# Layer 0 of a four-layer graph network: a hand-written order, one load per row tile, and the neighbour lists of two row tiles built later

## The chip, the cores and the metric

The kernel runs on one core of one Trainium2 chip. The number is device microseconds of one execution. The core has a matrix engine (TensorE, PE in the profile, its weight loads PEld), a vector engine (VectorE, DVE), an activation engine (ScalarE, ACT), a general engine (GpSimd, POOL), and a queue engine (SyncE, SP) that starts most transfers. Each works through its own instructions in order and waits on the others by semaphores.

## The reference, cut to what matters

`x` is 2708 x 128 and `adj` is 2708 x 2708, both float32. About 16 entries in a row of `adj` are not zero. Four layers follow each other, each of the form "normalise, ReLU, graph layer, add":

```python
# layer 0: aggregation over columns
h = relu(layernorm(x));  x = x + (adj.T @ h) / adj.sum(axis=0)[:, None]
# layer 1: one message for every pair (i, j), weighted with adj
h = relu(layernorm(x))
messages = gelu(s[:, None, :] + d[None, :, :] + msg_b)     # s, d: two linear maps of h
aggregated = einsum('ijd,ij->id', messages, adj)
x = x + layernorm(gelu(linear(h, aggregated)) + h)
# layer 2: adj @ h into a GRU cell;   layer 3: two heads of masked attention over adj
```

In layer 1 only the pairs with a non-zero entry count, so the kernel makes lists of these entries instead of computing 2708 x 2708 messages.

## The kernel before, in words

The rows of `adj` are cut into 22 row tiles of 128 (the last has 20), and the row tiles into six groups of four (`GROUPS`; the last group has tiles 20 and 21). The columns are cut into 22 blocks of `JB` = 124.

**Layer 0 (lines 227 to 290)** passes once over `adj` and does four things with each row tile:

- It adds to `adj.T @ h` on TensorE: six matmuls per tile into six PSUM banks (line 250).
- It lists the tile on VectorE: for each of the 22 blocks, line 269 (`nc.vector.max`) takes the eight largest values of each row and line 270 (`nc.vector.max_index`) their positions. The results are `val` and `col`. The two or three blocks around the diagonal come from a copy, `near`, in which GpSimd has put zeros on the diagonal (lines 259 and 262). GpSimd also makes `dg`, the diagonal alone (line 261). `near` and `dg` have two buffers each.
- ScalarE counts the entries of each row (line 274, `sign`) and takes the diagonal out of `dg` (line 275).
- When a group is complete, its four tiles are transposed block by block on TensorE into one of two PSUM banks (line 281), ScalarE copies the bank to `aT` with column sums (line 285), and SyncE stores it to `adjT` in device memory (line 288). `aT` has eight buffers. The sums of all 132 copies give the degrees.

Two groups of `adj` are held at a time (pool `l0`, `bufs=2`). The first and the last group are loaded tile by tile (line 244), the four in between with one transfer of 5.4 MB each (line 246). `moments_apart` computes the normalisation of the rows of tiles 4 to 21 on ScalarE and GpSimd. In this layer the order on each engine is found by a scheduler from priorities.

**The start of layer 1 (lines 738 to 751)** is a written order: `spread_sums` (line 676) transposes the sums, `enter` (line 685) divides them by the degrees and adds them to `x`, `count_rows` (line 362), `rank` (lines 377 to 379), `select_rows` (line 368), and so on until the loop can start.

**Layer 1's loop** is `period(t)`, 22 periods with one row tile each and six steps `k`. It is a pipeline: period `t` computes messages of tile `t` (`combine`, lines 528 and 532, and `gather`, line 553), and prepares tiles `t + 1` to `t + 4`. On VectorE a period has, in this order: `rank(t+3)` (lines 378, 379, from a PSUM bank that several small products share), `describe(t+3)` (line 354), `sources` in even periods (line 503), `select_rows(t+3)` (line 368), `count_rows(t+4)` (line 362, reads `val`), pieces of `update`, `columns(t+1)` (line 482), `place(t+2)` (lines 420 to 443) and `finish_rows(t+3)` (line 399). The order is written out, since the whole part stands under `tc.manual_schedule()`.

Layers 2 and 3 read `adjT` again and are not touched.

Of the kernel before, what the change touches and what calls it, by code (L numbers as in the profile page):

```python
# [20 lines left out]
F32 = mybir.dt.float32  # L21
BF16 = mybir.dt.bfloat16
AF = mybir.ActivationFunctionType
ALU = mybir.AluOpType
# [6 lines left out]
P = 128  # L31
N = 2708
D = 128
NT = (N + P - 1) // P
FULL = N // P
TAIL = N - FULL * P
CH = 512
CHUNKS = [(c, min(CH, N - c)) for c in range(0, N, CH)]
# [5 lines left out]
JB = 124  # L44
NB = (N + JB - 1) // JB
S = 8
E = P
GROUPS = [(t, min(4, NT - t)) for t in range(0, NT, 4)]
# [3 lines left out]
def size(t):  # L52
    return min(P, N - t * P)


def width(b):
    return min(JB, N - b * JB)
# [3 lines left out]
def listed_layers(ctx: ExitStack, tc: tile.TileContext, x, adj, w, out, flag):  # L61
    nc = tc.nc
# [7 lines left out]
    def bank(name):  # L70
        return ps.tile([P, CH], F32, tag="ps", name=name)

    xs = const.tile([P, NT, D], F32, name="xs")
    h = const.tile([P, NT, D], F32, name="hs")
    adjT = dram.tile([P, NT, N], F32, name="adjT")
# [10 lines left out]
    ident = const.tile([P, P], F32, name="ident")  # L86
# [47 lines left out]
    def scale_rows(dst, src, rstd, shift, func):  # L134

        for q in range(len(src)):
            nc.scalar.activation(dst[q], src[q], func, bias=shift[:, q : q + 1], scale=rstd[:, q : q + 1])

    def tiles_of(v, t, k):
        return [v[:, t + q, :] for q in range(k)]  # L140
# [50 lines left out]
    for q in range(2):  # L191
        nc.gpsimd.tensor_copy(xb[q][:, :, 4 * S : 4 * S + R], part.unsqueeze(1).to_broadcast([P, NB, R]))

    sumT = keep.tile([D, N], F32, name="hT1")
    hT = sumT
    with tc.tile_pool(name="l0c", bufs=1) as fix:
        offdiag = fix.tile([P, P], F32, name="offdiag")
        nc.vector.tensor_scalar(offdiag, ident, -1.0, 1.0, ALU.mult, ALU.add)  # L200
        sums = fix.tile([P, NT, len(GROUPS)], F32, name="sums")
        nc.gpsimd.memset(sums, 1.0)

        RT = NT - 4
        flat = fix.tile([P, 4, RT], F32, name="flat")
        shifts, ve, rstd, tmp = (flat[:, q, :] for q in range(4))

        def moments_apart(pool):
            for t in range(4, NT):
                junk = pool.tile([P, D], F32, name="junk")  # L210
                nc.scalar.activation(junk, xs[:, t, :], AF.Copy, accum_out=shifts[:, t - 4 : t - 3])
            nc.gpsimd.tensor_scalar(shifts, shifts, -1.0 / D, None, ALU.mult)
            for t in range(4, NT):
                junk = pool.tile([P, D], F32, name="junk")
                nc.scalar.activation(
                    junk, xs[:, t, :], AF.Square, bias=shifts[:, t - 4 : t - 3], accum_out=ve[:, t - 4 : t - 3]
                )
            nc.gpsimd.tensor_scalar(ve, ve, 1.0 / D, EPS, ALU.mult, ALU.add)
            nc.gpsimd.tensor_tensor(rstd, ve, minus_half[:, 0:RT], ALU.pow)
            nc.gpsimd.tensor_tensor(tmp, rstd, rstd, ALU.mult)  # L220
            nc.gpsimd.tensor_tensor(tmp, tmp, ve, ALU.mult)
            nc.gpsimd.tensor_scalar(tmp, tmp, -0.5, 1.5, ALU.mult, ALU.add)
            nc.gpsimd.tensor_tensor(rstd, rstd, tmp, ALU.mult)
            nc.gpsimd.tensor_tensor(shifts, shifts, rstd, ALU.mult)
            scale_rows(tiles_of(h, 4, RT), tiles_of(xs, 4, RT), rstd, shifts, AF.Relu)

        with (
            tc.tile_pool(name="l0", bufs=2) as rows,
            tc.tile_pool(name="l0k", bufs=2) as pool,
            tc.tile_pool(name="l0t", bufs=8) as turned,  # L230
            tc.tile_pool(name="l0p", bufs=1, space=PSUM) as acc,
        ):
            accs = [acc.tile([P, CH], F32, name=f"acc{c}") for c in range(len(CHUNKS))]
            for gi, (g0, gk) in enumerate(GROUPS):
                i0, iw = span(g0, gk)
                a4 = rows.tile([P, 4, N], F32, name="a")
                if gk < 4:
                    nc.gpsimd.memset(a4[:, gk - 1, :], 0.0)
                for q in range(gk):
                    n = g0 + q  # L240
                    m = size(n)
                    a = a4[:, q, :]
                    if not 0 < gi < len(GROUPS) - 1:
                        nc.sync.dma_start(a[0:m, :], adj[n * P : n * P + m, :])
                    elif q == 0:
                        nc.sync.dma_start(a4, adj[i0 : i0 + iw, :].rearrange("(t p) n -> p t n", p=P))
                    if n == 1:
                        load_rest()
                    for ci, (c, cw) in enumerate(CHUNKS):
                        nc.tensor.matmul(  # L250
                            accs[ci][:, 0:cw], h[0:m, n, :], a[0:m, c : c + cw], start=(n == 0), stop=(n == NT - 1)
                        )

                    d0 = n * P
                    b0 = d0 // JB
                    b1 = (d0 + m - 1) // JB
                    c0, c1 = b0 * JB, min((b1 + 1) * JB, N)
                    near = pool.tile([P, 3 * JB], F32, name="near")
                    nc.gpsimd.tensor_copy(near[:, 0 : c1 - c0], a[:, c0:c1])
                    dg = pool.tile([P, P], F32, name="dg")  # L260
                    nc.gpsimd.tensor_tensor(dg[:, 0:m], a[:, d0 : d0 + m], ident[:, 0:m], ALU.mult)
                    nc.gpsimd.tensor_tensor(
                        near[:, d0 - c0 : d0 - c0 + m], a[:, d0 : d0 + m], offdiag[:, 0:m], ALU.mult
                    )
                    for b in range(NB):
                        ab = a[:, b * JB : b * JB + width(b)]
                        if b0 <= b <= b1:
                            ab = near[:, b * JB - c0 : b * JB - c0 + width(b)]
                        nc.vector.max(val[:, n, b, :], ab)  # L269
                        nc.vector.max_index(col[:, n, b, :], val[:, n, b, :], ab)  # L270
                    if n == 2:
                        moments_apart(pool)
                    sign = pool.tile([P, N], BF16, name="sign")
                    nc.scalar.activation(sign, a, AF.Sign, accum_out=total[:, n : n + 1])
                    nc.scalar.activation(dg[:, 0:m], dg[:, 0:m], AF.Copy, accum_out=own[:, n : n + 1])
                for j in range(NT):
                    k = size(j)
                    p = bank("p_T")
                    for q in range(gk):
                        m = size(g0 + q)  # L280
                        nc.tensor.transpose(  # L281
                            p[0:k, q * P : q * P + m], a4[0:m, q, j * P : j * P + k], ident[0:m, 0:m]
                        )
                    aT = turned.tile([P, CH], F32, name="aT")
                    nc.scalar.activation(  # L285
                        aT[0:k, 0:iw], p[0:k, 0:iw], AF.Copy, accum_out=sums[0:k, j, gi : gi + 1]
                    )
                    nc.sync.dma_start(adjT[0:k, j, i0 : i0 + iw], aT[0:k, 0:iw])
            for ci, (c, cw) in enumerate(CHUNKS):
                nc.scalar.copy(sumT[:, c : c + cw], accs[ci][:, 0:cw])  # L290


        deg = fix.tile([P, 3, NT], F32, name="deg")
        dsum, lim, fin = (deg[:, q, :] for q in range(3))
        nc.vector.reduce_sum(dsum, sums, AX.X)
        nc.vector.reciprocal(inv, dsum)
        nc.vector.tensor_scalar(lim, inv, FMAX, -FMAX, ALU.min, ALU.max)
        nc.vector.tensor_tensor(fin, lim, inv, ALU.is_equal)
        nc.vector.tensor_tensor(inv, lim, fin, ALU.mult)
# [30 lines left out]
    with (  # L330
# [35 lines left out]
        def compare(dst, numbers, op):  # L366

            nc.vector.tensor_tensor(  # L368
                dst.rearrange("p b (x r) -> p b x r", r=R),
                count_h.rearrange("p (x r) -> p x r", r=R).unsqueeze(1).to_broadcast([P, NB, P // R, R]),  # L370
                numbers.unsqueeze(2).to_broadcast([P, NB, P // R, R]),
                op,
            )

        def rank(t):
            p = rpool.tile([P, CH], F32, tag="r", name="p_r")
# [20 lines left out]
        def finish_rows(t):  # L397
            sel = state[t]["sel"]
            nc.vector.tensor_tensor(sel, sel, later, ALU.subtract)
# [225 lines left out]
        def period(t, between=()):  # L625
# [5 lines left out]
            for k in range(GB):  # L631
# [33 lines left out]
                    place(t + 2)  # L665
                if k == 4 and a:
                    finish_rows(t + 3)


        def spread_sums(g):  # L670
# [946 lines left out]
```

## Time and profile before

| what | us |
|---|---|
| runs, median (lowest, highest) of 3 | 1091.82 (1085.76, 1094.81) |
| the profiled execution, and its span | 1090.83, 1089.0 |
| layer 0 up to the last list on VectorE | 0 to 223.4 |
| the last transposes and copies of layer 0 | 223.4 to 234.7 |
| start of layer 1 up to the first message products | 234.7 to 294 |
| layer 1's loop and its last updates | 294 to about 640 |
| layers 2 and 3 | about 640 to 1089 |

The table is cut by hand from the timelines. In the profile a group of instructions is one line: source line, engine, operation, output and input, shapes, count; then the busy time and the mean duration in ns; then the idle time of the engine just before these instructions and who ended it. The durations of neighbouring VectorE instructions overlap by a few tens of ns, so the pace of a sequence is read from start times.

### The profile page before, as it was taken

Reading aid. Unit: us, or ns where it says so; the run is one execution under the profiler, and the core shown is the slowest. Engines: PE = TensorE matmul, PEld = TensorE weight load, DVE = VectorE, ACT = ScalarE, POOL = GpSimd, SP = SyncE. Lnnn points to the kernel's source line nnn. Section 1 sums busy time; section 2 is a strip of 40 time slices with the busy share of each in tenths; the row PEclk is TensorE's granted clock in tenths of the full one; section 3 lists DMA queues with packets and bytes.
Section 4 is the critical chain, followed back from the end, with each engine's and each line's share of the span. In section 5 each row is a group of like instructions: output and inputs, shape, how many; then the busy total and the mean of one; then the engine's idle time right before and its main releaser. Section 6 shows DMA issues by size and latency. Waiting matters only on the chain. (4 is left out here: it accounts for less than half of the span.)

```text
span 1089.0 us, 21908 instructions
## 1 busy us (share of the span) xinstructions
PE 959.5 (88%) x7950; PEld 762.3 (70%) x7950; DVE 825.6 (76%) x2856; ACT 516.0 (47%) x1431; POOL 395.7 (36%) x474
## 2 busy tenths in 40 slices
PE   6688779964599999999999979999978999999993
PEld 3355445633499999989898944444578999999762
DVE  7999999957777667776887265666578977997673
ACT  7957547745566666666675522433322200230142
POOL 4301102012486655676666253444310300340132
PEclk9798899766599999999999989999989999899996
DMA  9586786441033322222222046556400000000000
GB/s 367 182 316 239 305 320 228 181 155 54 27 108 108 108 88 102 81 102 88 96 93 82 29 174 224 188 193 223 131 27 21 11 4 1 1 20 1 1 16 14
DMA packets 56922, 128.18 MB, mean 118 GB/s; under 512 B 7458, under 2 KB 20126, under 8 KB 54096
## 3 DMA queue, kind: packets, MB, share of 16 engines
q1 hardware_dynamic: 54988, 123.89, 32.2%
q10 hardware_dynamic: 1816, 2.80, 0.9%
q8 instruction: 64, 1.05, 0.4%
q14 instruction: 54, 0.44, 0.1%
HBM read 80.07 MB, written 30.87 MB: 102 GB/s over the span
## 5 line engine op out<-in xcount | busy, mean ns | idle before, releaser
L867 PE MATMUL att<-hv,wt 128*128 128x129 f32 (+2 forms) x1936 | 243.8, 283 | 8.8 <-DVE wt L835 8.8
L867 PEld LDWEIGHTS att<-hv,wt 128*128 128x128 f32 (+2 forms) x1936 | 224.7, 192 | 25.7 <-DVE wt L835 10.1
L835 DVE SCALAR_TENSOR_TENSOR wt<-row,lift,mask 128x1024 f32<-128x1024 f32 (+5 forms) x176 | 160.2, 939 | 35.0 <-PE att L867 35.0
L452 POOL TENSOR_SCALAR put<-mine,value 128x128 f32<-128x128 bf16 x176 | 148.2, 858 | 72.4 <-DVE mine L368 70.0
L528 PE MATMUL p_m<-s,sel 128*128 128x128 bf16 x1452 | 161.6, 220 | 5.5 <-ACT g L540 5.5
L532 PE MATMUL p_m<-d,cols 124*128 124x128 bf16 (+1 forms) x1452 | 161.7, 219 | 1.4 <-DVE cols L482 1.3
L121 POOL TENSOR_TENSOR n_r<-n_r,minus_half 128x4 f32<-128x4 f32 (+1 forms) x31 | 46.1, 1488 | 304.5 <-DVE n_r L120 298.9
L250 PE MATMUL acc<-a,hs 128*128 128x512 f32 (+2 forms) x264 | 119.0, 589 | 26.6 <-DMA a<-in_adj 22.7
L553 PE MATMUL agg<-put,g 128*128 128x128 f32 (+1 forms) x968 | 135.8, 281 | 0.0
L270 DVE FIND_INDEX8 col<-val,a 128x8 uint16<-128x124 f32 (+1 forms) x441 | 118.6, 281 | 0.0
L553 PEld LDWEIGHTS agg<-put,g 128*128 128x128 f32 x968 | 118.1, 192 | 0.0
L1006 PE MATMUL p_agg<-a,hs 128*128 128x512 f32 (+2 forms) x264 | 111.0, 563 | 7.8 <-DVE u L601 4.8
L528 PEld LDWEIGHTS <-sel 128*128 128x128 bf16 x1452 | 104.2, 98 | 10.9 <-issue 7.1
L269 DVE MAX8 val<-a 128x8 f32<-128x124 f32 (+1 forms) x441 | 102.6, 273 | 2.2 <-DMA a<-in_adj 2.2
L532 PEld LDWEIGHTS <-cols 124*128 124x128 bf16 (+1 forms) x1452 | 102.4, 98 | 1.9 <-DVE cols L482 1.9
L540 ACT ACTIVATE g<-p_m 128x512 f32<-128x512 f32 x132 | 73.1, 554 | 63.4 <-PE p_m L532 63.4
L281 PEld LDWEIGHTS p_T<-ident,a 128*128 128x128 f32 x484 | 61.8, 152 | 57.7 <-ACT aT L285 34.0
L460 ACT ACTIVATE put<-mine,value 128x128 f32<-128x128 bf16 x308 | 100.4, 390 | 0.0
L281 PE MATMUL p_T<-ident,a 128*128 128x128 f32 x484 | 80.7, 302 | 19.5 <-DMA a<-in_adj 10.1
L250 PEld LDWEIGHTS acc<-a,hs 128*128 128x128 f32 (+1 forms) x264 | 48.0, 204 | 66.4 <-issue 38.6
L1006 PEld LDWEIGHTS p_agg<-a,hs 128*128 128x128 f32 (+1 forms) x264 | 48.2, 196 | 57.0 <-issue 56.0
L285 ACT ACTIVATE aT<-p_T 128x512 f32<-128x512 f32 (+2 forms) x132 | 71.0, 544 | 32.5 <-issue 13.9
(244 smaller groups left out, 1401.8 us busy)
## 6 DMA issues: line engine op xcount, KB each, us to landing
adjT<-aT SPq DMA_DIRECT2D x105, 256.0 KB
a<-adjT SPq DMA_DIRECT2D x20, 1280.0 KB
a<-in_adj SPq DMA_DIRECT2D x4, 5416.0 KB
spread<-passed SPq DMA_DIRECT2D x22, 704.0 KB
later<-sel SPq DMA_DIRECT2D x22, 616.0 KB
a<-in_adj SPq DMA_DIRECT2D x5, 1354.0 KB
row<-own_d ACTq DMA_DIRECT2D x10, 256.0 KB
later<-sel SPq DMA_DIRECT2D x22, 82.5 KB
```

The lines of the kernel that those rows point to most:

```text
L250: nc.tensor.matmul(accs[ci][:, 0:cw], h[0:m, n, :], a[0:m, c : c + cw], start=(n == 0), stop=(n == NT - 1))
L269: nc.vector.max(val[:, n, b, :], ab)
L270: nc.vector.max_index(col[:, n, b, :], val[:, n, b, :], ab)
L281: nc.tensor.transpose(p[0:k, q * P : q * P + m], a4[0:m, q, j * P : j * P + k], ident[0:m, 0:m])
L452: nc.gpsimd.tensor_scalar(st["put", 0][:, b, :], st["mine"][:, b, :], st["value"][:, b : b + 1], None, ALU.mult)
L460: nc.scalar.activation(st["put", 1][:, b - HP, :], st["mine"][:, b, :], AF.Identity, scale=st["value"][:, b : b + 1])
L528: nc.tensor.matmul(p[:, b - b0, :], st["sel"][:, b, :], s3[:, q, t % 2, :], start=(q == 0), stop=False)
L532: nc.tensor.matmul(p[:, b - b0, :], st["cols"][0:kb, b, :], d3[0:kb, b, q, :], start=False, stop=(q == 2))
L553: nc.tensor.matmul(agg, g[:, b - 4 * k, :], put, start=(b == 0), stop=False)
L835: nc.vector.scalar_tensor_tensor(wt[0:kj, :], row[0:kj, k, c : c + n], lift[0:kj, j, k : k + 1], mask[0:kj, j, c : c + n], op0=ALU.max, op ...
L867: nc.tensor.matmul(banks[s // 3][0:m, s % 3, :], wt[0:kj, q * P : q * P + m], hv[0:kj, j, k, :], start=(v < 2 and s // 3 not in touched), ...
L1006: nc.tensor.matmul(pa[:, 0:n], h[0:k, j, :], a[0:k, j - j0, 0:n], start=(j == 0), stop=(j == NT - 1))
```

## The change

It rewrites layer 0 as small functions called in a written order, loads every row tile with a transfer of its own, and moves most of the lists of tiles 20 and 21 into layer 1's loop. For that those blocks of `adj` are read a second time.

- `LATER` is 20: of tiles 20 and 21 only the blocks around the diagonal are listed in layer 0. The other 20 + 21 = 41 blocks go into `late_blocks`.
- `load_late(t + 1)` stands in period `t` at `k == 4` and loads three blocks of 128 x 124 (20 x 124 for tile 21) into `cols_a` (two buffers). `list_late(t)` stands at the end of period `t`, behind `finish_rows`, and lists those three. Periods 1 to 14 have such blocks.
- Row tile loads of group `g + 1` stand between the transposed blocks of group `g`, at `j` = 3, 7, 11, 15.
- In groups 1 to 4, the matmuls of `adj.T @ h` are spread between the transposes of the same group, about one after each block. In the first and the last group they come ahead of the transposes.
- In a list, the blocks around the diagonal come last, and pairs of blocks are taken together.
- The copies of the six sums (`sumT`) come after all transposes.

```diff
+    LATER = NT - 2
+    AT_ONCE = 3
+    late_blocks = []
+    nc.gpsimd.memset(val[:, NT - 1, :, :], 0.0)
+    nc.gpsimd.memset(col[:, NT - 1, :, :], 0.0)
...
+            def list_row_tile(n):
...
+                blocks = [b for b in range(NB) if not b0 <= b <= b1] + list(range(b0, b1 + 1))
+                if n >= LATER:
+                    late_blocks.extend((n, b) for b in range(NB) if not b0 <= b <= b1)
+                    blocks = range(b0, b1 + 1)
+                for k in range(0, NB, 2):
+                    for b in blocks[k : k + 2]:
+                        nc.vector.max(val[:, n, b, :], block(b))
+                    for b in blocks[k : k + 2]:
+                        nc.vector.max_index(col[:, n, b, :], val[:, n, b, :], block(b))
...
+            with tc.manual_schedule():
+                for n in range(8):
+                    load_row_tile(n)
                     if n == 1:
                         load_rest()
...
+                for gi, (g0, gk) in enumerate(GROUPS):
+                    steps = [(n, ci) for n in range(g0, g0 + gk) for ci in range(len(CHUNKS))]
+                    ahead = gi == 0 or gk < 4
+                    for n in range(g0, g0 + gk):
+                        if ahead:
+                            for ci in range(len(CHUNKS)):
+                                aggregate_rows(n, ci)
+                        if n < 2:
+                            list_row_tile(n)
+                            sign_sums(n)
+                            (sum_rows, sum_squares)[n](pool)
+                    done = 0
+                    for j in range(NT):
+                        turn_blocks(gi, j)
+                        now = len(steps) * (j + 1) // NT
+                        for step in steps[done:now]:
+                            if not ahead:
+                                aggregate_rows(*step)
+                        done = now
+                        n = g0 + j // 5
+                        if j % 5 == 1 and j // 5 < gk and n > 1:
+                            list_row_tile(n)
+                        if j % 5 == 3 and j // 5 < gk and n > 1:
+                            sign_sums(n)
+                        if gi > 0 and j % 4 == 3 and j < 16 and g0 + 4 + j // 4 < NT:
+                            load_row_tile(g0 + 4 + j // 4)
+                        if j == NT - 2 and gi + 1 < len(GROUPS):
+                            normal_rows(gi + 1)
+                for ci, (c, cw) in enumerate(CHUNKS):
+                    nc.scalar.copy(sumT[:, c : c + cw], accs[ci][:, 0:cw])
...
+        def load_late(t):
+
+            units = late_blocks[(t - 1) * AT_ONCE : t * AT_ONCE] if t > 0 else []
+            if not units:
+                return
+            cols = work.tile([P, AT_ONCE, JB], F32, name="cols_a")
+            state["late", t] = []
+            for i, (n, b) in enumerate(units):
+                m, k = size(n), width(b)
+                nc.sync.dma_start(cols[0:m, i, 0:k], adj[n * P : n * P + m, b * JB : b * JB + k])
+                state["late", t].append((n, b, cols[0:m, i, 0:k]))
+
+        def list_late(t):
+            units = state.pop(("late", t), [])
+            for n, b, a in units:
+                nc.vector.max(val[0 : size(n), n, b, :], a)
+            for n, b, a in units:
+                nc.vector.max_index(col[0 : size(n), n, b, :], val[0 : size(n), n, b, :], a)
...
                 if k == 4 and a:
                     finish_rows(t + 3)
+                if k == 4:
+                    load_late(t + 1)
+                if k == GB - 1:
+                    list_late(t)
```

## The prediction

> **What bounds the kernel now.** I read the slices of the page first, then VectorE's timeline in layer 0, then the end of layer 0, then VectorE's gaps in layer 1. VectorE in forty slices of 27 us:
>
> ```profile
> DVE  7999999957777667776887265666578977997673
> PEclk9798899766599999999999989999989999899996
> ```
>
> It is full from the second slice to the eighth and never again. Its timeline there shows nothing but lists, with no idle time in any row from 7.4 to 223.4 us:
>
> ```profile
> 102.71 0.46 DVE L269 MAX8 val<-a 128x8 f32<-128x124 f32 x2
> 103.09 0.07 DVE L270 MATCH_VALUE_LOAD col<-val,a 128x8 f32 x1
> 103.15 0.28 DVE L270 FIND_INDEX8 col<-val,a 128x8 uint16<-128x124 f32 x1
> 103.35 0.07 DVE L270 MATCH_VALUE_LOAD col<-val,a 128x8 f32 x1
> 103.41 0.28 DVE L270 FIND_INDEX8 col<-val,a 128x8 uint16<-128x124 f32 x1
> 103.61 0.27 DVE L269 MAX8 val<-a 128x8 f32<-128x124 f32 x1
> ```
>
> Two blocks start at 102.71 and the next two at 103.61: 0.445 us a block, 9.8 us a row tile, 39.2 us a group; 484 blocks are 215.4 us. After the last block VectorE waits 11 us for the last copy of a transposed block (ScalarE, ends 234.6; I call this time T), and the start of layer 1 hangs on it:
>
> ```profile
> 234.40 0.25 DVE L362 TENSOR_SCALAR some<-val 128x176 bf16<-128x176 f32 x1 [11.04 <-ACT aT L285]
> ```
>
> In layer 1's loop TensorE is the bound. Stages from the windows view (PE, PEld, DVE, ACT, POOL busy; clock; DMA share; GB/s):
>
> ```profile
> 125.00:164.00 39.00, 31.26 (x136) 18.76 (x134) 39.00 (x265) 23.71 (x60) 4.27 (x11) 0.89 0.74 279
> 294.00:605.00 311.00, 300.26 (x4188) 289.32 (x4187) 229.25 (x438) 203.34 (x597) 205.53 (x259) 0.99 0.27 93
> ```
>
> In a group of layer 0 only VectorE is full; in the loop TensorE has 97% and VectorE 74%. So work is moved from where VectorE is the bound to where it isn't.
>
> **Part 1: what leaves layer 0.** 41 blocks x 0.445 = 18.2 us. Tile 21's last block now ends at 223.4 - 18.2 = 205.2 us, if VectorE still never waits; tile 19, ahead of three diagonal blocks (1.3 us), at 203.9.
>
> **Part 2: can VectorE start to wait?** Three new ways, each with its cover.
> - Loads: tiles 8 to 11 are issued around 60 us, when group 1 is being transposed, and listed from 86. In the profile 5.4 MB took up to 18 us beside the stores (issue 146.1, matmuls go on at 164.2). Cover 8 us; cost 0, up to 3. The extra loads' issue on SP, 12 x 0.4 us, lies in a queue that waited 127 us for ScalarE.
> - GpSimd's queue: `near` of tile 2 now stands behind the normalisation chain, which waits for ScalarE's 18 squares. ScalarE: first `sign` ends 9.9, four rows, `dg`, 18 sums (5.3 us), second `sign` 2.6, 18 squares (6.9): about 28 us; the chain's 5.0 us (29.7 to 34.7 before): 33; `near` 0.9: 34. VectorE wants it at about 37.5, since diagonal blocks now come last. Cost 0, up to 2. The two new memsets (about 0.5 us estimated from the 0.21 us row of `sums`) lie ahead of the first `near`, with 8 us of cover.
> - `near` of tile n waits for VectorE to end tile n - 2, `dg` comes behind it and ScalarE's `sign` step waits for `dg`. So TensorE and ScalarE can't run more than two tiles ahead, and VectorE leads them.
>
> **Part 3: the end of layer 0, the new T.** Two paths.
> - By VectorE: tile 19 ends 203.9; `near` and `dg` of tile 21 (0.27 + 0.23 + 0.23 at 203.7 before) 204.6; ScalarE's `dg` 0.4; then 13 block copies. Before, the 22 of this group took 12.6 us, 0.57 each: 7.4. T = 212.4.
> - By TensorE: `dg` of tile 19 follows the end of tile 17 (184.3), so ScalarE passes it at 186; three blocks and two rows: 189.5; then 12 matmuls ahead of the transposes. At full speed they take 0.43 us (two in 0.86 us, 140.66 to 141.52), at half speed 0.945 (four in 3.78 us after a wait): 4.6 to 10.5, I take 7: 196.5. Then 22 x 0.57, two `sign` (2.5 each), two `dg` (0.4): 18.3. T = 214.8.
>
> The later one holds: T = 214.8, from 212.4 to 218.3. Gain 234.6 - 214.8 = **19.8 us**.
>
> **A rule that speaks against it.** TensorE's need per group is 88 transposes and 24 matmuls. At full speed (8 transposes and two matmuls in 1.73 us, around 140 us in the timeline) that is 88 x 0.11 + 20 x 0.43 + 4 x 0.17 = 19 us; at half speed (8 transposes in 1.97 us at 42.75) 88 x 0.25 + 20 x 0.945 + 4 x 0.5 = 43 us, more than VectorE's 39.2. The Trainium skill, page "TensorE: Matmul & The Clock Gate", Part 1, says that about 3.4 us without work halves the clock and about 3.4 us of steady work restores it; Part 4 adds that transposes don't count as work. The new order has only bursts of four transposes and one matmul, and ScalarE's `sign` and `dg` (3 us) stop them in every tile, with more waiting for VectorE. By the rule alone TensorE would stay at half speed: four groups x 3.8 us late, T = 230. The trace agrees that waits of 7 us halve the speed, but the same mixture with waits of 0.2 to 0.4 us ran at full speed, and a TensorE that is late has no long waits, so it recovers. I take the row, and keep the rule as a rival.
>
> **Part 4: the start of layer 1 loses some.** Before, sums were copied at 204 to 213, and `spread_sums` was done before T. Now the six copies (0.5 us each) come after T, then eight transposes in a row (2.1 us at half speed), then `rank`'s product, and VectorE takes `rank`'s result ahead of `enter`. Its first `enter` was T + 2.2 before. Now: bank freed by the third or fourth copy, T + 2, transposes T + 4.2, product and copies T + 5. So 2.7 us late; lower end 0 (the inverse degrees alone need 2.2), upper 4. The rest of the start (59 us) keeps its order.
>
> **Part 5: the lists in the loop.** Three blocks are 1.34 us, 18.2 us in all, in periods 1 to 14, behind `finish_rows` and ahead of the next `rank` copies, `v_r`, `sel`. Queued behind them is everything VectorE owes TensorE. The gaps there:
>
> ```profile
> 343.89 0.18 DVE L378 CAST ends<-p_r 128x22 bf16<-128x22 f32 x1 [0.19 <-PE p_r L377]
> 345.03 0.34 DVE L354 TENSOR_TENSOR v_r<-val,xb 128x176 f32<-128x176 f32 x1 [0.81 <-ACT xb L353]
> 357.71 0.18 DVE L378 CAST ends<-p_r 128x22 bf16<-128x22 f32 x1 [3.43 <-PE p_r L377]
> ```
>
> Even periods start with 2.3 to 3.4 us of waiting and take 1.34 whole. Odd ones have 0.2 to 0.8, then 0.81 ahead of `v_r`: they end up to 0.4 us late, and the next even period's gap takes that. Only around periods 10 to 12 VectorE is late already (TensorE waited 0.81 us for `sel` at 465.9 and 0.63 for `cols` at 460.4): about 0.4 us lost there. With ScalarE's `xb` late in six periods I take **1 us**, from 0 to 5. Reading 1.5 MB again (20 blocks of 63.5 KB, 21 of 9.9) lies beside a DMA share of 0.27 and lands 14 us before use: 0.
>
> **Sum:** -19.8 + 2.7 + 1 = -16.1 on the profiled 1090.8: **1074.7 us**, rounded 1075. The profiled execution is 1.0 below the median, so that is 1.5% under 1091.8. Its own range by the ends kept: gain 22.2 - 0 - 0 to 16.3 - 4 - 5, so 1068.6 to 1083.5, and 1067 to 1084 with the runs' scatter.
>
> **Rivals.**
> - A (above), chance 0.72.
> - B: TensorE stays at half speed and becomes layer 0's bound. For: 43 against 39.2, and a clock of 0.89 even now. Against: the 19 us at full speed. T = 230: gain 4.6, less 3.7 lost later: 1090, within 1%. With half of that effect 1082. Chance 0.16.
> - C, slower: the lists in the loop are stretched while GpSimd works. VectorE rows do stretch there (`mine` 2.53 us against 1.61; a 128x4 product at 271.73 1.11 against 0.16), and GpSimd is busy 66% of the loop. If each of the six list instructions took 0.9 us more, a period's lists would cost 6.7 us: odd periods have about 2.2 us of gaps, even ones 7, so seven odd periods lose 4.5 us each, 31 us, and the end is 1090.8 - 17.1 + 31 = 1105. It decides above 17.1/7 + 2.2 = 4.6 us per period. Against: the lists ran at 0.28 us beside GpSimd's work at 193.3 too. Chance 0.05.
> - D: VectorE gets starved in layer 0 (loads or `near` late in each group by 3 us): five groups, 15 us, 1090. Against: Part 2's covers. Chance 0.07.
>
> **Chances.** About 1% (10.9 us) is what a measurement of this kernel tells from no change; the line is 1080.9. Faster: A without the 0.05 of it that lies above the line, half of B (0.08), and 0.02 of D: 0.77. Slower by over 1%: C, and 0.01 of D: 0.06. Within 1%: the rest, 0.17. The range takes A nearly whole, and half of B and of D: 1067 to 1087.
>
> **What would show it.** The last list of layer 0 at 205 us with no VectorE gap before; last `aT` copy at 212 to 218; first `enter` about 5 us after it; list rows in the loop at 0.28 us; loop pace as before (13.8 to 16 us a period). A granted clock under 0.7 with TensorE full in layer 0 is B; list rows above 0.6 us is C; VectorE gaps behind loads or `near` are D.

## The result, and the profile after

| | before | after |
|---|---|---|
| median (lowest, highest) of the runs beside each other | 1091.25 (1085.76, 1094.81), 4 runs | 1076.88 (1076.27, 1077.95), 4 runs |
| profiled execution, and its span | 1090.83, 1089.0 | 1077.95, 1076.2 |
| last list of layer 0 ends | 223.4 | 205.5 |
| T, the last `aT` copy (start of the read of its sum) | 234.6 | 219.97 |
| first `enter` starts | 236.77 | 225.12 |
| last `n1u` factors of layer 1's updates | 643.8 | 632.61 |

After over before is 0.9874, with a 95% interval of 0.9831 to 0.9916: 1.3% faster. (A ratio need not be the quotient of the two medians.) More executions later gave 1076.25 (1073.6 to 1077.12, 6 runs), ratio 0.9864 [0.9839, 0.9889]. The forecast was 1075.

The timeline of the changed kernel around the end of layer 0 (start, us, engine, line, operation, names, count, and in brackets the idle time ahead and who ended it):

```profile
190.03 11.37 PE L296 MATMUL acc<-a,hs 128*128 128x512 f32 x28
...
202.11 0.29 ACT L312 ACTIVATE aT<-p_T 128x148 f32<-128x148 f32 x1 [10.68 <-issue]
...
205.21 0.26 DVE L284 FIND_INDEX8 col<-val,near 128x8 uint16<-128x104 f32 x1
219.80 0.25 DVE L421 TENSOR_SCALAR some<-val 128x176 bf16<-128x176 f32 x1 [14.32 <-ACT aT L312]
...
222.75 1.97 PE L758 MATMUL p_m<-ident,hT 128*128 128x128 f32 x8 [3.16 <-ACT hT L349]
...
224.87 0.18 DVE L456 CAST ends<-p_r 128x22 bf16<-128x22 f32 x1 [2.98 <-PE p_r L455]
225.12 0.34 DVE L767 SCALAR_TENSOR_TENSOR xs<-p_m,inv_deg,xs 128x128 f32<-128x128 f32 x1
```

Three things are to be seen. VectorE ends its lists at 205.5 as forecast, but the next row shows that it then stands for 14.32 us, longer than the 11.04 before: 18 us were taken off VectorE and it is no nearer to being the bound here. What it waits for is ScalarE, and ScalarE itself stood for 10.68 us, exactly while TensorE ran products (the first row; its 28 records are 14 products, the last two of tile 19 and the twelve of tiles 20 and 21). And behind T come the copies of the sums and eight transposes, until `enter` starts at 225.12.

In layer 1's loop, one odd and one even period:

```profile
332.53 0.66 DVE L449 MAX8 val<-cols_a 128x8 f32<-128x124 f32 x3
...
333.88 0.17 DVE L456 CAST ends<-p_r 128x22 bf16<-128x22 f32 x1
...
346.42 0.18 DVE L456 CAST ends<-p_r 128x22 bf16<-128x22 f32 x1 [2.04 <-PE p_r L455]
```

The lists run at the pace of layer 0 and take 1.34 us (332.53 to 333.88, where `rank`'s copy follows without a wait). In the even period 2.04 us of waiting are still left in front of `rank`'s copy.

### The profile page after: what moved, and what is told of

Its sections match the earlier page's. It is cut to its first block, busy times and chain, and to the rows that moved or that the text cites. A ratio compares the mean times of both kernels' runs of the same rounds, so it can differ in the third digit from the quotient of the medians.

```text
span 1076.2 us, 21996 instructions
## 1 busy us (share of the span) xinstructions
PE 950.2 (88%) x7950; PEld 756.6 (70%) x7950; DVE 824.4 (77%) x2856; ACT 516.5 (48%) x1431; POOL 398.0 (37%) x476
## 5 line engine op out<-in xcount | busy, mean ns | idle before, releaser
L296 PE MATMUL acc<-a,hs 128*128 128x512 f32 (+2 forms) x264 | 119.8, 563 | 11.1 <-ACT hs L137 11.1
L308 PE MATMUL p_T<-ident,a 128*128 128x128 f32 x484 | 84.3, 295 | 30.9 <-ACT aT L312 23.5
L284 DVE FIND_INDEX8 col<-val,a 128x8 uint16<-128x124 f32 (+1 forms) x400 | 109.2, 290 | 0.0
L282 DVE MAX8 val<-a 128x8 f32<-128x124 f32 (+1 forms) x400 | 94.2, 282 | 2.1 <-DMA a<-in_adj 2.1
L296 PEld LDWEIGHTS acc<-a,hs 128*128 128x128 f32 (+1 forms) x264 | 44.6, 199 | 31.2 <-issue 19.9
```

Of the source, the lines that this page charges most:

```text
L282: nc.vector.max(val[:, n, b, :], block(b))
L284: nc.vector.max_index(col[:, n, b, :], val[:, n, b, :], block(b))
L296: nc.tensor.matmul(accs[ci][:, 0:cw], h[0:m, n, :], sets[n // 4][0:m, n % 4, c : c + cw], start=(n == 0), stop=(n == NT - 1),)
L308: nc.tensor.transpose(p[0:k, q * P : q * P + m], sets[gi][0:m, q, j * P : j * P + k], ident[0:m, 0:m])
```

## Experiments

The letters A to F of this section are its own, not the rivals of the prediction. Theory A at the outset: TensorE and ScalarE end layer 0, so the written order brings the gain, and the lists bring little. Rival B: the 18.2 us that leave VectorE are the gain. Two executions of the same layer 0 can differ by 3 us in T (219.97 above, 216.70 and 217.24 below), so differences of a few us are read from T onwards, in the traces. T is given as in the table.

### 1 and 2. Either half of the change alone

```diff
-    LATER = NT - 2
+    LATER = NT
```

> The changed kernel without late lists (LATER = NT): the written order and the single loads stay, and all 484 blocks are listed in layer 0 again. Theory A, the written order brings the gain: the last aT copy stays at about 220 us, because it was TensorE and ScalarE that set it; VectorE ends its lists at 205.5 + 41 x 0.445 = 223.5, 3.5 us behind the last copy, so the first enter moves from 225.1 to about 226.5, and the loop gives back 0.4: 1078, from 1077 to 1080. Rival B, the 18.2 us taken off VectorE bring the gain: 1090, no better than before.

Measured: 1082.55 us (8 runs), ratio 0.993 [0.9905, 0.9955]. T was 220.07, where it is with the late lists. VectorE's rows and the first `enter`:

```profile
223.24 0.28 DVE L284 FIND_INDEX8 col<-val,near 128x8 uint16<-128x104 f32 x1
223.42 0.25 DVE L421 TENSOR_SCALAR some<-val 128x176 bf16<-128x176 f32 x1
...
225.66 0.34 DVE L767 SCALAR_TENSOR_TENSOR xs<-p_m,inv_deg,xs 128x128 f32<-128x128 f32 x1
```

VectorE now lists until 223.5 and goes on without a wait. Against the execution of the table above, `enter` is only 0.54 us later than with the late lists, period 0's `rank` copy 1.9 (292.31 against 290.39), the last updates 2.2. But that execution is the slowest of the changed kernel's ten. Against its second trace (experiment 7; T = 216.70, first `enter` at 221.85) `enter` is 3.8 us later and the last updates 4.7 (634.77 against 630.11). The runs say 5.7 to 6.3 us, and the time missed the expected 1077 to 1080. So I count the lists at 2 to 5 us by the traces and at most 6 by the runs; the difference between the two lies in layers 2 and 3, whose code is the same.

The other half is the kernel before, with the late blocks left out of its loop over `b`, and `load_late` and `list_late` in `period`:

```diff
+                        if n >= LATER and not b0 <= b <= b1:
+                            late_blocks.append((n, b))
+                            continue
                         ab = a[:, b * JB : b * JB + width(b)]
```

> The kernel before with the late lists alone: 41 blocks of tiles 20 and 21 leave layer 0 and are listed three per period in layer 1, order and loads as before. Theory A: VectorE ends layer 0 at about 205.5, but the last aT copy stays at 234 to 235, since TensorE and ScalarE set it; enter follows 2 us later as before, the loop costs 0.4: 1091, from 1088 to 1093. Rival B: the last copy moves forward with VectorE, 1073 to 1077.

Measured: 1088.56 us (20 runs) against 1090.89; ratio 0.999 [0.9975, 1.0005], no difference told.

```profile
205.13 0.26 DVE L281 FIND_INDEX8 col<-val,near 128x8 uint16<-128x104 f32 x1
238.21 0.25 DVE L373 TENSOR_SCALAR some<-val 128x176 bf16<-128x176 f32 x1 [32.81 <-ACT aT L296]
```

VectorE ends 18 us sooner and waits 32.81 us: the whole saving is turned into idle time. (Its T of 238.4 is late even for this kernel; the profiled execution, 1092.5, is one of its slowest.) **B falls.** The order and the loads without the lists have 8 of the 14 us, the lists without them 0 to 2; together they have more than the sum.

### 3. The loads: how much of "the order" are they?

Groups 1 to 4 loaded with 5.4 MB at a time again:

```diff
-                        if gi > 0 and j % 4 == 3 and j < 16 and g0 + 4 + j // 4 < NT:
-                            load_row_tile(g0 + 4 + j // 4)
+                        if gi > 0 and j == 3 and gi + 1 < len(GROUPS):
+                            load_group(gi + 1)
```

> The changed kernel with the rows of groups 1 to 4 loaded as in the kernel before, 5.4 MB in one transfer, issued at the fourth block of the group ahead (the written order otherwise kept; tiles 20 and 21 one after the other at that block). Theory A, it is the order and not the size of the loads: TensorE waits 2 to 3 us per group or less for rows, last aT copy at 217 to 221, 1077 (1074 to 1080). Rival F, the single loads make the gain: TensorE waits some 7 us per group as in the kernel before, last copy at 225 or later, 1083 or more.

Measured: 1086.14 us (20 runs), ratio 0.9968 [0.9954, 0.9983], 10 us above the changed kernel; T = 227.08. Rival F holds for the time, and my theory that the loads hardly matter fell. But F's mechanism is not what the trace shows. SyncE's queue, and ScalarE, in the second group:

```profile
59.90 0.38 SPq L263 DMA_DIRECT2D a<-in_adj  x1
62.69 17.52 SPq L323 DMA_DIRECT2D adjT<-aT  x9
...
79.17 0.60 ACT L322 ACTIVATE aT<-p_T 128x512 f32<-128x512 f32 x1 [7.64 <-DMA adjT<-aT]
```

and ScalarE's copies over layer 0 (busy, mean ns of one | idle before, and the releasers), of this kernel:

```profile
L322 ACT ACTIVATE aT<-p_T 128x512 f32<-128x512 f32 (+2 forms) x132 | 71.1, 541 | 60.4 <-ACT aT L322 24.7 <-DMA adjT<-aT 21.6 <-issue 9.7
```

and of the changed kernel:

```profile
L312 ACT ACTIVATE aT<-p_T 128x512 f32<-128x512 f32 (+2 forms) x132 | 71.1, 541 | 52.8 <-ACT aT L312 27.6 <-issue 20.6 <-PE p_T L308 4.7
```

Nobody waits for the rows in the big-load version. ScalarE waits three times (7.6, 6.4, 7.5 us) for one of the eight `aT` buffers, whose store was issued behind the big load; TensorE then waits for ScalarE's bank (5.70, 4.50 and 5.55 us at 79.92, 116.94 and 155.23). With single loads ScalarE has no wait for a store that shows. Instead TensorE waits 2.1 to 2.7 us per group for the last row tile of the next. In the kernel before, TensorE waits 6.8 to 7.7 us per group for the rows themselves, as F had it. One such wait of each, first with big loads, then of the changed kernel, then of the kernel before:

```profile
79.92 1.12 PE L318 MATMUL p_T<-ident,a 128*128 128x128 f32 x4 [5.70 <-ACT aT L322]
...
89.27 0.33 PE L308 MATMUL p_T<-ident,a 128*128 128x128 f32 x1 [2.55 <-DMA a<-in_adj]
...
85.08 3.78 PE L250 MATMUL acc<-a,hs 128*128 128x512 f32 x4 [7.69 <-DMA a<-in_adj]
```

By the end of group 4 this has added up: the 28 records that start at 190.03 in the changed kernel start at 198.19 with big loads. The edit changes two things at once, the size of a load and its moment (all of a group at one block, in place of one tile at each of four blocks); which of them matters is not shown.

### 4. Twice the lists in the loop

```diff
             units = state.pop(("late", t), [])
+            units = units + units
```

> The changed kernel with every late block listed twice in the loop, 2.68 us a period in place of 1.34 (18.2 us more on VectorE in periods 1 to 14). Theory A, the loop is TensorE's and VectorE has 2 to 3 us of waits in every second period: the first 1.34 cost 0.4 us in all, the second takes the odd periods' too: 3 to 9 us more, 1080 to 1086. Rival: lists in the loop are not hidden and each us costs one: 1095.

Measured: 1077.53 us (4 runs), ratio 0.9887 [0.9844, 0.9929]. T was 217.24. From period 0's `rank` copy to the last updates the kernel before takes 341.8 us, the changed kernel 342.2 (343.0 in another execution), this one 345.5. The two versions of the new order without late lists (experiments 1 and 8) take 342.5 and 342.2. So the lists cost the loop at most 1.2 us and perhaps nothing, and as much again costs another 2.5 to 3.3: the lower end of A's 3 to 9, and far from the 18 of the rival. The time lies under the expected 1080 to 1086; T was early in this execution.

### 5. The products of the last two tiles among group 4's blocks

```diff
-                    steps = [(n, ci) for n in range(g0, g0 + gk) for ci in range(len(CHUNKS))]
-                    ahead = gi == 0 or gk < 4
+                    last = NT if gi == len(GROUPS) - 2 else g0 + gk
+                    steps = [(n, ci) for n in range(g0, last) for ci in range(len(CHUNKS))]
+                    ahead = gi == 0
+                    steps = steps if gk == 4 else []
```

(`normal_rows(5)` moves to the end of group 3.)

> The changed kernel with the 12 products of tiles 20 and 21 spread over group 4's blocks in place of ahead of group 5's transposes. Theory A: what holds the last aT copy back is the 11.4 us (190.0 to 201.4) in which TensorE runs these 12 products and ScalarE stands; spread they fill TensorE's waits of group 4 in part (10.3 us of work into some 5 us of waits), so the last copy comes at 213 to 215 and the time falls by 5 to 7: 1070 to 1072. Rival D: the end of layer 0 is held by the dg of tile 21, which follows VectorE's end of tile 19 at 203.9: last copy 212.4 at the earliest, nothing to tell from A, but ScalarE then stands ahead of the dg. Rival E: the start of layer 1 doesn't follow the last copy: 1077.

Measured: 1075.05 us (4 runs, 1070.87 to 1080.86), not told from the changed kernel; the expected 1070 to 1072 was missed. (The profiled execution was the fastest of the four.) T = 215.36, 1.3 to 4.6 earlier than in executions of the changed kernel, just behind the 213 to 215 that I expected. The 12 products no longer stand ahead of the transposes, but the granted clock, the share of full speed that the profile shows for TensorE, was at a mean of 0.52 from 194 to 196, still during the products of tile 21, and the 22 blocks of group 5 then take 0.63 us each. That led to the next question.

### 6. Products over 20 rows and the clock

Tile 21 has 20 rows, so its products use 20 of 128 partitions. The edit gives them all 128, of which 108 are zeros (`h` and `a` are zero there):

```diff
-                    accs[ci][:, 0:cw], h[0:m, n, :], sets[n // 4][0:m, n % 4, c : c + cw],
+                    accs[ci][:, 0:cw], h[:, n, :], sets[n // 4][:, n % 4, c : c + cw],
```

> The changed kernel with tile 21's six products over all 128 rows (108 of them zeros) in place of 20, nothing else. If products over 20 rows let the clock fall, it now stays at 1.00 through the 12 products: 10.3 us in place of 11.4, and a few us of group 5's transposes at full speed too; from the first of the 12 products to the last aT copy 28 us in place of 30.1, last copy 215 to 218, about 1074.5. Rival: the clock falls anyway, 30 us and 1076.

The windows view of TensorE (us, busy and count, granted clock, DMA share, GB/s), first of the changed kernel:

```profile
196.00:198.00 2.00, 2.00 (x5) 1.00 0.00 0
198.00:200.00 2.00, 2.00 (x6) 0.91 0.00 0
200.00:202.00 2.00, 2.00 (x7) 0.50 0.00 0
```

and with 128 rows:

```profile
198.00:200.00 2.00, 1.80 (x9) 1.00 0.25 76
200.00:202.00 2.00, 0.31 (x2) 1.00 0.25 76
```

and TensorE's timeline with 128 rows:

```profile
187.22 10.36 PE L296 MATMUL acc<-a,hs 128*128 128x512 f32 x28
197.41 2.89 PE L308 MATMUL p_T<-ident,a 128*128 128x128 f32 x12
```

In the changed kernel the products over 20 rows begin at 195.77, TensorE is busy without a break, and the clock falls at about 199.6 (a window mean of 0.91 is 1.00 for 1.64 us and 0.50 for the rest). With 128 rows it stays at 1.00 through the products and 5 us beyond; the same row of 28 records takes 10.36 in place of 11.37 us and the first 12 transposes 2.89 in place of 3.83 (201.33 in the changed kernel). From the start of that row to T it is 28.2 us in place of 29.9, as expected. The time is 1074.31 us (5 runs), ratio 0.9865 [0.9833, 0.9897]: 2 us under the changed kernel's, where it was expected, but too little for these runs to tell. What the clock does is shown by the trace, what it is worth in the whole time is not.

### 7. The sums copied by VectorE

Experiment 5 with the six copies of the sums on VectorE, which is idle; then the same with tile 21's products over 128 rows; then the first without late lists:

```diff
-                    nc.scalar.copy(sumT[:, c : c + cw], accs[ci][:, 0:cw])
+                    nc.vector.tensor_copy(sumT[:, c : c + cw], accs[ci][:, 0:cw])
```

> The products of tiles 20 and 21 spread over group 4, and the six copies of the sums written for VectorE in place of ScalarE, where they lie in its idle time behind the lists (205.1 to about 209) and no longer behind the last aT copy. Last aT copy at 214 to 216 as with the spreading alone; if the start of layer 1 was late because of these copies, the first enter comes 2.2 to 2.8 us behind it in place of 5.0, and the time falls by 7 from the changed kernel's: 1070, from 1067 to 1073. Rival: the inverse degrees, the rank product and its copies hold enter at 4.5 us or more whatever the copies do: 1072 to 1075, the time of the spreading alone.

> As the last one, and tile 21's six products over all 128 rows (108 of them zeros) in place of 20. In four traces the granted clock fell to 0.50 some 3.6 to 3.9 us after the products over 20 rows began, with TensorE never idle. If it is the few rows that let the clock fall, it stays at 1.00 through these products and falls only during the transposes of group 5: about 1 us off the products, 1 to 2 off the transposes, last aT copy at 212 to 214, 1068 (1065 to 1071). Rival: the clock falls at the same time whatever the rows, for a reason of its own: no difference.

> As the spreading with the copies on VectorE, without late lists (all 484 blocks in layer 0). Theory A: what the lists are worth depends on how far VectorE is behind the last aT copy. Here VectorE ends its lists at 223.5 and copies sums until 227, against a last aT copy at 215: first enter at 228 to 229 in place of 218, 10 us later: 1080, from 1077 to 1083. Rival: the lists are worth the 4 us at most that they brought with the order of the changed kernel: 1074.

All three missed: 1081.55 us (ratio 0.9916 [0.9892, 0.9939]), 1081.43 (0.9912 [0.9889, 0.9936]) and 1100.85 (1.0094 [1.0069, 1.0118], slower than before), six runs each. T was 225.5, 225.4 and 243.6. Beside them the changed kernel itself had 1076.25 and T = 216.70:

> The changed kernel itself once more, beside the next three on the same chip, because its executions so far are few and two executions of one and the same layer 0 (this kernel's and that of the one with double lists) had their last aT copy at 220.1 and 217.4. Expected: 1077, from 1075 to 1080, last aT copy anywhere from 217 to 221, first enter 5 us behind it.

TensorE and VectorE of the first:

```profile
205.19 3.28 DVE L353 COPY hT<-acc 128x512 f32<-128x512 f32 x6
...
202.07 1.95 PE L308 MATMUL p_T<-ident,a 128*128 128x128 f32 x6
208.52 0.48 PE L762 MATMUL p_m<-ident,hT 128*128 128x128 f32 x1 [4.50 <-DVE hT L353]
208.79 0.64 PE L308 MATMUL p_T<-ident,a 128*128 128x128 f32 x2
```

TensorE of the third:

```profile
226.58 0.48 PE L762 MATMUL p_m<-ident,hT 128*128 128x128 f32 x1 [28.03 <-DVE hT L353]
```

`p_m`, the transposes of `spread_sums`, which belong to layer 1, now stand in TensorE's queue behind the third block of group 5. In experiment 5, where ScalarE makes the copies, all eight stand behind the last block. So a written order holds within its own part of the program, but the next part's instructions can start among these, and where they do changed when the copies changed their engine. That the scheduler chose it is my inference. TensorE's queue then stood until VectorE had ended its lists and six copies (205.19 + 3.28 = 208.47): 4.50 us in the first, 14.20 in the second, where TensorE came there 10 us sooner for nothing, and 28.03 in the third, where the lists go on until 223.3. The second's clock stayed at 1.00 until about 196.7 with 128 rows, as experiment 6 has it; in the first the mean from 194 to 196 was 0.54. So the times of these three say nothing about what the copies after T cost. But `enter` came 2.1 us behind T (225.50 to 227.64 in the first), about as expected, now that neither the copies nor `p_m` stand behind T. And they show what a VectorE that is late costs once something of TensorE's waits for it.

### 8. A better version, with and without the late lists

Experiments 5 and 6 together; `near` and `dg` with three buffers; the copies of the sums on ScalarE, one behind each of the last six blocks of group 5:

```diff
-                for ci, (c, cw) in enumerate(CHUNKS):
-                    nc.scalar.copy(sumT[:, c : c + cw], accs[ci][:, 0:cw])
+                        if gi == len(GROUPS) - 1 and j >= NT - len(CHUNKS):
+                            c, cw = CHUNKS[j - NT + len(CHUNKS)]
+                            nc.scalar.copy(sumT[:, c : c + cw], accs[j - NT + len(CHUNKS)][:, 0:cw])
```

> The products of tiles 20 and 21 spread over group 4; tile 21's over all 128 rows; near and dg of three buffers (so that the dg of tile 21 waits for VectorE's end of tile 18, not 19); the six copies of the sums on ScalarE, one behind each of the last six blocks of group 5. TensorE ends its products at about 193, the blocks and two signs follow without a wait, last aT copy at 210 to 213, first enter 2.2 to 2.8 us behind it at 213 to 216, against 222 to 225 in the changed kernel: 1067, from 1063 to 1071. Rival: the clock or the planner takes it back, last copy at 215 or later: 1072 or more.

> As the last one, without late lists. The sums are copied by ScalarE here, so nothing of TensorE's waits for VectorE. VectorE ends its lists at 223.5, 12 us behind the last aT copy: first enter at 225.5 to 226.5, 1079 (1076 to 1082), 12 more than with the late lists, where the same lists were worth 4 to 6 with the changed kernel's order. Rival: they are worth the same 4 to 6 us in any order: 1072.

Measured: 1069.01 us (6 runs), ratio 0.9822 [0.979, 0.9854], against 1080.15 (5 runs), 0.991 [0.988, 0.994]. Of the better version:

```profile
193.20 2.90 PE L309 MATMUL p_T<-ident,a 128*128 128x128 f32 x12
...
211.35 0.25 DVE L427 TENSOR_SCALAR some<-val 128x176 bf16<-128x176 f32 x1 [6.14 <-ACT aT L313]
...
214.61 1.12 DVE L773 SCALAR_TENSOR_TENSOR xs<-p_m,inv_deg,xs 128x128 f32<-128x128 f32 x4
```

The transposes of group 5 start at 193.20 in place of 201.33, T is 211.85, and `enter` follows 2.8 us behind it in place of 5.1. (What the third buffers of `near` and `dg` bring alone was not run.) Without the late lists T is 214.2 and VectorE is busy until `enter`:

```profile
223.06 0.26 DVE L285 FIND_INDEX8 col<-val,near 128x8 uint16<-128x104 f32 x1
223.24 0.23 DVE L427 TENSOR_SCALAR some<-val 128x176 bf16<-128x176 f32 x1
...
225.46 1.12 DVE L773 SCALAR_TENSOR_TENSOR xs<-p_m,inv_deg,xs 128x128 f32<-128x128 f32 x4
```

`enter` comes 10.9 us later and the time is 11.1 us longer, as theory A had it (12). The same lists were worth 0 to 2 us in the order of before, 2 to 6 in the order of the changed kernel, and 11 here: their worth is how far VectorE's end lies behind the other engines' end, and the earlier these end, the more of the 18.2 us counts.

## Why the prediction was right, point by point

- **What bounds layer 0:** the prediction opens with VectorE as the only full engine and takes the gain from moving its work. That step failed where it matters, at the end of layer 0: with the order and loads of before, the same 41 blocks moved gained 0 to 2 us, and VectorE waited 32.81 us for ScalarE (experiment 2). A full engine need not be the one whose end the next stage waits for. The forecast did not depend on it, because Part 3 works out both paths and takes the later one, which is TensorE's.
- **Part 1, last list at 205.2 us without a gap:** 205.5, and no gap in the rows of the lists. Right.
- **Part 2, VectorE isn't starved:** right; the only wait in front of a list row is 2.1 us for the first rows of `adj`. GpSimd's and ScalarE's new places cost VectorE nothing.
- **Part 3, T = 214.8, gain 19.8:** T was 219.97, gain 14.6, outside its own 212.4 to 218.3 in this execution (216.70 and 217.24 in two others). The path was right: TensorE's, not VectorE's. The step that failed is "12 matmuls ahead of the transposes. At full speed they take 0.43 us (...): 4.6 to 10.5, I take 7". Each product leaves two records in the trace: line 296 has 264 of them for 132 products. The prediction took the spacing of records for that of products. The row of 11.37 us holds two products of tile 19, 0.86 and 0.42, so the twelve ran from 191.3 to 201.3: 10.0 us for the forecast 7. With the clock at 1.00 throughout (experiment 6) they take 10.36 - 1.28 = 9.1, so the ends should have been 9.1 and some 21 (20 x 0.945 + 4 x 0.5). Of the 5.2 us missed, 3.0 are this term, 1.8 the start (191.3 for 189.5, of which the last two products of tile 19 are 1.3), and 0.3 the blocks and signs behind (18.6 for 18.3).
- **The clock rule against the row:** the same slip makes the group's sum too small: 88 x 0.11 + 20 x 0.86 + 4 x 0.42 (a short product is two records in 0.42) = 29 us at full speed, not 19, and about 64 at half speed, not 43: rival B would have cost some 25 us a group, not 3.8. The choice of the row was right nevertheless. Two groups of the changed kernel (PE, PEld, DVE, ACT, POOL busy; clock; DMA share; GB/s):

```profile
98.00:133.00 35.00, 28.89 (x137) 17.12 (x136) 35.00 (x239) 26.92 (x67) 4.24 (x10) 1.00 0.89 320
133.00:168.00 35.00, 28.88 (x136) 17.11 (x136) 35.00 (x237) 27.48 (x70) 6.57 (x13) 1.00 0.91 324
```

  Full clock through bursts of four transposes and one product. The corrected 29 us is what TensorE is busy. Where there were only transposes the rule of the Trainium skill (page "TensorE: Matmul & The Clock Gate", Part 4, transposes don't count as work) agrees with the trace of the better version:

```profile
192.09 1.28 PE L297 MATMUL acc<-a,hs 128*128 128x512 f32 x4
...
196.00:198.00 2.00, 0.09 (x1) 0.74 0.25 73
```

  The last product ended at 193.4, transposes ran until 196.1, and the clock fell at about 197.0 (a window mean of 0.74), 3.6 us behind the product and only 0.9 behind the transposes. (In experiment 6 and in the better version without late lists it fell 5 and 6 us behind the last product.) Rival B would have needed longer gaps between products than the mixture had.
- **Part 4, the start of layer 1 loses 2.7:** `enter` came 5.1 us behind T for the forecast 5. Right, and the cause too: with the copies among the last blocks it was 2.8 (experiment 8).
- **Part 5, 1 us for the lists in the loop:** 0 to 1.2. Right; rival C, stretched lists, did not happen (1.34 us for three blocks).
- **The sum:** -14.6 + 3.0 + 0.4 make -11.2 at the last updates (643.8 to 632.61); the span is 12.8 shorter, and 1.6 of that lie in layers 2 and 3, which the change doesn't touch. Forecast -16.1. So by this trace the forecast is 5 us too good at the last updates, by the second (630.11) 2.4; that the median of the runs lies within 2 us of 1075 is in part luck.
- **What the prediction did not see:** Part 3 lets TensorE's path start when VectorE has passed tile 17, so it takes it without a reason that TensorE and ScalarE keep up until there. They do so only with the single loads, to which it gives no gain: with big loads the 28 records start 8 us later, and the same order and the same lists gain 4 of the 14 us (experiment 3).

## What to carry to other kernels

Work that is taken off the busiest engine is worth only as much as that engine's end lies behind the end of the others: find the second latest engine before counting, and count again when another edit moves it (here 0 to 2, 2 to 6 and 11 us for the same 41 blocks). A large load can hurt through what is queued behind it: in experiment 3 the waits were for stores that give buffers back and none was for the load itself, and single loads in its place still gained 10 us. Before a duration is multiplied by a count of instructions, divide the trace's count of records by the program's count of instructions.

## What was not expected of the hardware

- Products over 20 of 128 partitions did not hold the clock. In the five traces where they stand in one row it fell to 0.50 while TensorE was busy without a break, 3.6 to 5.3 us after the first of them (changed kernel 195.77 to 199.6, again 192.97 to 197.3, order alone 195.58 to 199.2, double lists 192.94 to 196.7, big loads 203.93 to 209.2). With zeros in the other 108 rows it stayed at 1.00 through all of them, in four traces. In the five traces where transposes stand between these products (the kernel before among them) it fell as well, some 2.5 to 6 us after the first. Why is not shown, nor where between 20 and 128 rows the line lies.
- Stores of 256 KB issued behind a load of 5.4 MB held ScalarE up to 7.6 us although `aT` has eight buffers; with loads of 1.35 MB, spread over the group, no such wait is in the trace.
